# Product 4 of the first layer through seven products of its own blocks

## The chip, the cores and the metric

The kernel runs on one core of a Trainium2 chip. The metric is device time in microseconds (us) of one execution; lower is better. Five engines work side by side, each through its own queue in order: TensorE (PE, matrix products; its weight loads are listed as PEld), VectorE (DVE), ScalarE (ACT), GpSimd (POOL, which also issues indirect DMAs) and SyncE (SP, which here only issues DMAs). Products are written to eight banks of 128x512 float32 in PSUM; everything else lies in SBUF. An instruction that needs another engine's result waits for it on a semaphore, and what stands behind it in its queue waits too.

## The reference

4096 tokens of 512 columns are rotated by quaternions (which reduces to a mixture of four blocks of 128 columns with 16 weights each) and sent through a mixture of 8 experts, two per token, with 1024 slots per expert.

```python
x_rotated = hamilton(q_left_n, hamilton(x_filtered, q_right_conj))
scores = softmax(xf @ gate_w.T);  topv, topi = top_k(scores, 2)
gates = topv / sum(topv)
disp[flat_idx] += xf * w                       # 8 experts x 1024 slots x 512
h = relu(einsum('ecd,ehd->ech', de, fc1_w) + fc1_b)     # 2048 hidden units
eo = einsum('ech,ehd->ecd', h, fc2_w) + fc2_b
out = x + sum(eo[flat_idx] * gates * w)
```

All data are float32. Most of the work is in the two products of each expert: 1024 slots x 512 x 2048, twice.

## The kernel before

After the routing (some 80 us, with the DMAs that it waits for) the kernel goes through 32 groups k = 4e+g: expert e, group g of 512 hidden units. A group's first layer multiplies weights (two blocks of 256 hidden units by two blocks of 256 columns) with slots (two halves of 512 slots). It does so by seven block products in place of eight (the form of Strassen and Winograd), numbered 0 to 6: left[i] is a block of the weights or a sum of blocks, right[i] a block or sum of blocks of the slots. `left1` makes four such sums per group on POOL, s0 to s3; `Slots.factors` makes four per expert, on POOL too (x0 to x3, 1024 columns each, by `sums`, lines 125 to 128). The results are four blocks of hidden units by slots, called h11, h21, h22 and r12, made of bank contents: product 0 with the bias gives h11; product 5 on top of it r12 and h21; 1 is added to h11; 6 to h21; 4 to h22 and to r12; 3 and 2 to h21 and r12.

Products 0, 5 and 4 are done directly (`half`, line 858): two halves m of 128 hidden units, two steps c of 128 columns, 128x512 each. Products 1, 6, 3 and 2 are done by seven products of their own blocks once more (`within`, line 837): 128x128 by 128x256, with sums of sums made by `left_sub` (POOL, lines 155 to 158, 128 columns each, four per group and product) and `right_sub` (DVE, lines 170 to 173, 256 columns each, four per expert and product). `pair` does two such products side by side, (1, 6) and (3, 2), so that one DVE addition (line 892) adds one bank to two result blocks; a bank t is accumulated on and read four times in turn, a bank u twice. Where a bank is written again, TensorE waits for the addition that reads it. After the two pairs, `chain` puts four DVE sums of 1024 columns (lines 820 to 825) at the front of the queue `background`; they make the left sides of the second layer.

The second layer (`second_layers`, `product2`, line 800) takes the group before, in two units of 256 slots, each with seven products of 128x128 by 128x256 four times, and additions into `acc` on DVE.

The order is written out by hand. The two generators are stepped in turn, 14 turns per group: a step of the first layer (for a direct product one half, for a pair two to four small products) and then one step of the second (one product). After each step `turn(n)` takes n entries of `background` (rotation of the next expert's slots, line 771 and the transposes of line 727; storing of results) and one of `fetches` (indirect gathers on POOL, lines 601, 633 and 694; exchanges of 32-column squares by SP, line 707, four DMAs an entry). `PACE` gives n by group, turn and generator. `TURN_OF_SUM` gives the turn of each of the four left sums, and the tuples behind `left_sub` and `right_sub` the turns of their four steps. The next expert's slots are gathered, exchanged, rotated and summed during groups 0 to 3 of the present one; its four sums x0 to x3 stand at turns 10 to 13 of group 3.

Memory for the hidden blocks: `beside` holds three blocks of a group next to each other (h11, h21, r12) in two copies, `unused` five single blocks, from which h22 and the sums of `chain` are taken and to which `product2` returns them.

Of the kernel before, what the change touches and what calls it, by code (L numbers as in the profile page):

```python
# [30 lines left out]
F32 = mybir.dt.float32  # L31
# [4 lines left out]
ALU = mybir.AluOpType  # L36
# [30 lines left out]
def kernel(  # L67
# [546 lines left out]
    beside = [hp.tile([P, 3, 2, HALF], F32, name=f"beside{i}") for i in range(2)]  # L614
    unused = [hp.tile([P, 2, HALF], F32, name=f"hidden{i}") for i in range(5)]
# [60 lines left out]
    class Slots:  # L676
# [37 lines left out]
        def arrivals(self, half):  # L714

            n = PER if half == 0 else 2
            t = self.a if half == 0 else self.b
            for at in range(0, PER, n):
                for st in range(n):
                    yield lambda st=st, at=at: self.gather_ahead(t[:, st], half, at + st)  # L720
                yield from [lambda: None] * 2
                for b in range(QT):
                    yield lambda b=b, at=at: self.exchange(t, half, at, b)
                yield from [lambda: None] * 2
# [71 lines left out]
    def product2(out, st0, factors, n, first, tiles=range(2)):  # L796
# [11 lines left out]
        if st0 + 2 == PER and 1 in tiles and n in (2, 3, 4, 5):  # L808
            unused.append(factors[0][n])

    def chain(k, h22):


        h11, h21, r12 = (beside[k % 2][:, i] for i in range(3))
# [3 lines left out]
        def last():  # L818
# [7 lines left out]
            *[lambda: None] * (2 if k == NK - 1 else 0),  # L826
            last,
        ]

# [16 lines left out]
    def layer1(k, factors, subs):  # L846
# [5 lines left out]
        h11, h21, r12 = (h[:, i] for i in range(3))  # L852
# [25 lines left out]
        def pair(n, o, at, base, base_read):  # L878

            two = h[:, at : at + 2]
            t, u = bank1(f"t{n}_{k}"), bank1(f"u{n}_{k}")
            halves = t.rearrange("p (n s) -> p n s", n=2)

            def both(bank, i, first=False):
                within(bank[:, A], subs, n, i, first)
                within(bank[:, B], subs, o, i)

            def add(m, half):  # L890
                to = two[:, :, m, half]
                V.tensor_tensor(to, halves, to, ALU.add)  # L892

            within(base[:, A], subs, o, 1)
            within(base[:, B], subs, o, 2)
            base_read()
            both(t, 0, True)
            add(0, A)
            yield
            both(t, 5)  # L900
            add(0, B)
            both(u, 4, True)
            to = two[:, :, :, B]
            term = u.rearrange("p (n s) -> p n s", n=2).unsqueeze(2).to_broadcast([P, 2, 2, HS])
            V.tensor_tensor(to, term, to, ALU.add)
            yield
            both(t, 6)
            add(1, B)
            within(u[:, A], subs, n, 1, True)
            within(u[:, B], subs, n, 2)  # L910
            V.tensor_tensor(two[:, 0, 0], u, two[:, 0, 0], ALU.add)
            yield
            both(t, 3)
            add(1, A)
            relu(two[:, 0])

        def from5(m):
            nc.scalar.activation(h21[:, m], a[m], AF.Identity, bias=hi[:, m : m + 1])

        def from4(m):  # L920
            V.tensor_tensor(r12[:, m], b[m], r12[:, m], ALU.add)

        yield from pair(1, 6, 0, a[0], lambda: from5(0))
        yield
        h22 = unused.pop(0)
        b = [bank1(f"b{m}_{k}") for m in range(2)]
        for m in range(2):
            half(b[m], m, 4, True)
            V.tensor_tensor(h22[:, m], b[m], h21[:, m], ALU.add)
            if m == 1:  # L930
                from4(1)
                relu(h22)
            yield
# [378 lines left out]
```

## Time and profile before

| | us |
|---|---|
| median of 3 runs (lowest to highest) | 1564.13 (1563.52 to 1565.92) |
| the profiled execution, whole | 1567.49 |
| its span, first to last instruction | 1565.7 |
| VectorE busy | 1152.8 |
| GpSimd busy | 1045.9 |
| one group of hidden units (stretch from 360.50 to 407.00) | 46.5 |

A profile's page gives busy time by engine, the chain of work that ended last, and groups of equal instructions: line, engine, operation, output from inputs, shape, count, then busy us and mean ns of one, then the engine's idle us in front of them with what ended it. Answers in order of time have the start in us, the duration in us, engine, line, operation and what it writes from what; in square brackets the idle time before and who ended it. A float32 product appears as two passes. Consecutive passes overlap in this list, so a pass's cost is the distance between starts and not its duration.

### The profile page before, as it was taken

To read this page: it belongs to the slowest core of one execution; us is meant where nothing else is said; L and a number is where in the kernel's file an instruction comes from. 1 tells how busy PE (TensorE), PEld (TensorE's weight loads), DVE (VectorE), ACT (ScalarE), POOL (GpSimd) and SP (SyncE) were. 2 spreads that over 40 slices of the span, in tenths; PEclk is the share of its full clock that TensorE was granted. 3 is DMA by queue.
4 is the path that set the end of the run, shared out by engine and by line. 5 is a ranking of instruction groups with operands and counts; after the bars stand their busy time and mean duration, and the time that the engine had idled before them with its cause. 6 is when DMAs were issued, how large, how long until landed. Compare 5 with 4: busy or idle time off the path is not lost.

```text
span 1565.7 us, 17505 instructions
## 1 busy us (share of the span) xinstructions
PE 1531.0 (98%) x6399; PEld 1186.9 (76%) x6399; DVE 1152.8 (74%) x1608; ACT 316.6 (20%) x446; POOL 1045.9 (67%) x1129
## 2 busy tenths in 40 slices
PE   5899999999999999999999999999999999999997
PEld 2677777877877777877877777887777877777776
DVE  6667887588866888578885888758886688866656
ACT  3222211211131211221122221221212211121110
POOL 1763687755977478865779567785687747886453
PEclk7899999999999999999999999999999999999999
DMA  8463113421335203441135311442123511321021
GB/s 325 150 215 101 55 61 122 121 81 55 96 106 144 65 28 114 124 118 55 54 95 166 96 55 32 137 130 86 55 79 115 145 41 55 114 94 67 0 82 53
DMA packets 79374, 152.18 MB, mean 97 GB/s; under 512 B 12022, under 2 KB 40950, under 8 KB 74168
## 3 DMA queue, kind: packets, MB, share of 16 engines
q1 hardware_dynamic: 56848, 90.24, 18.6%
q0 software_dynamic: 18048, 52.31, 10.8%
q10 hardware_dynamic: 4392, 8.52, 1.4%
q8 instruction: 50, 0.82, 0.2%
q14 instruction: 36, 0.29, 0.1%
HBM read 119.77 MB, written 25.23 MB: 93 GB/s over the span
## 4 chain that ended last, share of the span: by engine, by line
PE 87%; DVE 6%; DMA 2%; issue 2%; POOL 1%; another core or an unknown queue 1%; SPq 1%; POOLq 0%; DVEq 0%
PE a L800 26%; PE b L800 19%; PE t L837 13%; PE a L858 11%; PE u L837 7%; PE b L858 7%; PE b L837 2%; PE a L837 1%; DMA xb<-in_xt_dram 1%; DVE hidden L824 1%; DVE xa L771 1%; PE p L959 1%; DVE hidden L820 1%; SPq L707 1%
## 5 line engine op out<-in xcount | busy, mean ns | idle before, releaser
L800 PE MATMUL a<-t,hidden 128*128 128x256 f32 x1024 | 242.0, 379 | 0.1
L892 DVE TENSOR_TENSOR beside<-t,beside 128x512 f32<-128x512 f32 x248 | 170.3, 687 | 92.3 <-PE t L837 88.1
L800 PEld LDWEIGHTS a<-t,hidden 128*128 128x128 f32 x1024 | 194.5, 190 | 53.0 <-issue 27.5
L833 ACT ACTIVATE beside<-beside 128x1024 f32<-128x1024 f32 x62 | 65.5, 1057 | 556.8 <-DVE beside L892 535.1
L837 PE MATMUL t<-xsub,sub 128*128 128x256 f32 x496 | 128.1, 381 | 0.9 <-DVE beside L892 0.2
L800 PEld LDWEIGHTS b<-w,hidden 128*128 128x128 f32 x504 | 95.8, 190 | 39.0 <-issue 29.2
L800 PE MATMUL b<-w,beside 128*128 128x256 f32 x512 | 121.0, 379 | 0.6 <-DVE acc L1224 0.6
L800 PE MATMUL a<-t,beside 128*128 128x256 f32 x512 | 120.9, 379 | 0.0
L800 PE MATMUL a<-w,beside 128*128 128x256 f32 x512 | 120.9, 379 | 0.0
L800 PE MATMUL b<-t,hidden 128*128 128x256 f32 x504 | 119.1, 379 | 0.0
L800 PE MATMUL b<-w,hidden 128*128 128x256 f32 x504 | 119.1, 379 | 0.0
L800 PEld LDWEIGHTS b<-w,beside 128*128 128x128 f32 x512 | 97.2, 190 | 27.3 <-issue 15.8
L800 PEld LDWEIGHTS a<-w,beside 128*128 128x128 f32 x512 | 97.3, 190 | 26.4 <-issue 14.8
L858 PE MATMUL b<-x,s 128*128 128x512 f32 x248 | 116.5, 592 | 0.0
L858 PE MATMUL a<-x,s 128*128 128x512 f32 x248 | 116.5, 592 | 0.0
L858 PE MATMUL a<-xa,w 128*128 128x512 f32 x248 | 116.4, 592 | 0.0
L137 POOL TENSOR_TENSOR s<-w 128x512 f32<-128x512 f32 x31 | 39.5, 1274 | 112.5 <-PE b L858 112.5
L139 POOL TENSOR_TENSOR s<-w 128x512 f32<-128x512 f32 x31 | 39.7, 1282 | 109.7 <-PE t L837 109.6
L140 POOL TENSOR_TENSOR s<-w,s 128x512 f32<-128x512 f32 x31 | 39.4, 1272 | 107.5 <-PE t L837 96.7
L800 PEld LDWEIGHTS a<-t,beside 128*128 128x128 f32 x512 | 97.3, 190 | 13.2
L837 PEld LDWEIGHTS t<-xsub,sub 128*128 128x128 f32 x496 | 93.6, 190 | 16.3 <-DVE beside L892 3.4
L800 PEld LDWEIGHTS b<-t,hidden 128*128 128x128 f32 x504 | 95.8, 190 | 13.0
(228 smaller groups left out, 3084.9 us busy)
## 6 DMA issues: line engine op xcount, KB each, us to landing
w<-in_w_dram SPq DMA_DIRECT2D x64, 1024.0 KB
xb<-in_xt_dram SPq DMA_DIRECT2D x8, 1024.0 KB
out_dram<-in_x_dram ACTq DMA_DIRECT2D x1, 8192.0 KB
rows<-xa SPq DMA_DIRECT2D x112, 64.0 KB
rows<-xb SPq DMA_DIRECT2D x224, 32.0 KB
b<-in_b_dram POOLq DMA_DIRECT2D x8, 256.0 KB
c<-choice,slot_cho POOLq DMA_INDIRECT x64
rows<-out_dram,slot_tok POOLq DMA_INDIRECT x64
```

The source lines that it names most:

```text
L137: lambda: G.tensor_tensor(s[0], w[:, 1, 0], w[:, 1, 1], ALU.add),
L139: lambda: G.tensor_tensor(s[2], w[:, 0, 0], w[:, 1, 0], ALU.subtract),
L140: lambda: G.tensor_tensor(s[3], w[:, 0, 1], s[1], ALU.subtract),
L707: nc.sync.dma_start(slots_of[half][q * CW : (q + 1) * CW, at : at + t.shape[1], b * P : (b + 1) * P], t[b * CW : (b + 1) * CW, :, q * P : ...
L771: V.scalar_tensor_tensor(to, t, M[:, i, j : j + 1], to, ALU.mult, ALU.add)
L800: nc.tensor.matmul(out[m] if isinstance(out, list) else out[:, m], lhsT=factors[0][n][:, c, (st0 + m) * P : (st0 + m + 1) * P], rhs=factor ...
L820: V.tensor_tensor(s4, h21, s2, ALU.subtract)
L824: lambda: V.tensor_tensor(s2, s1, h11, ALU.subtract),
L833: nc.scalar.activation(h, h, AF.Relu)
L837: nc.tensor.matmul(out, lhsT=subs[0][n][i], rhs=subs[1][n][i], start=first, stop=True, skip_group_check=True,)
L858: nc.tensor.matmul(out, lhsT=factors[0][n][:, c, m * P : (m + 1) * P], rhs=factors[1][n][:, c, :], start=first and c == 0, stop=c == 1, sk ...
L892: V.tensor_tensor(to, halves, to, ALU.add)
```

## The change

Product 4 is taken out of the direct products. Its blocks now come from `left_sub` and `right_sub` too (four more sums of 128 columns on POOL per group, four more of 256 columns on DVE per expert), and it is done by `within` in seven products of 128x128 by 128x256. Two banks serve it: b takes products 1 and 2 of its blocks (and afterwards those of product 2), t4 the others, its first half in four steps one after the other, its second half in one. h22 becomes a fourth block of `beside`, so that one DVE addition of a t4 half reaches h22 and r12 together (`add_to_both`); ACT copies the second half of h21 to h22 beforehand. In turn 9 both products into t4 stand in front of the additions that read them.

Around it: `unused` shrinks from five blocks to three; the last sum of `chain` is held in `waiting` until the second layer's unit returns its block, after that unit's product 2; left sums 0 and 1 move to turns 11 and 12, since s0 is read until turn 11; the steps of `left_sub` and `right_sub` are placed anew (in an expert's first group the sums of slots stand in turns 2 to 10); gathers and exchanges of the next expert are appended part by part at the turns of `ARRIVE`, and its rotation starts at turn 7 of group 1 and turn 6 of group 2; `PACE` is rewritten, and group 1 of the whole run uses the row of its own position.

```diff
-    beside = [hp.tile([P, 3, 2, HALF], F32, name=f"beside{i}") for i in range(2)]
-    unused = [hp.tile([P, 2, HALF], F32, name=f"hidden{i}") for i in range(5)]
+    beside = [hp.tile([P, 4, 2, HALF], F32, name=f"beside{i}") for i in range(2)]
+    unused = [hp.tile([P, 2, HALF], F32, name=f"hidden{i}") for i in range(3)]
...
-        def arrivals(self, half):
+        def arrive(self, half, part):
...
-            for at in range(0, PER, n):
-                for st in range(n):
-                    yield lambda st=st, at=at: self.gather_ahead(t[:, st], half, at + st)
-                yield from [lambda: None] * 2
-                for b in range(QT):
-                    yield lambda b=b, at=at: self.exchange(t, half, at, b)
-                yield from [lambda: None] * 2
+            at = part // 2 * n
+            if part % 2 == 0:
+                return [
+                    lambda st=st: self.gather_ahead(t[:, st], half, at + st) for st in range(n)
+                ]
+            return [lambda b=b: self.exchange(t, half, at, b) for b in range(QT)]
...
-        if st0 + 2 == PER and 1 in tiles and n in (2, 3, 4, 5):
+        if st0 + 2 == PER and 1 in tiles and n in (2, 4, 5):
...
-    def chain(k, h22):
-        h11, h21, r12 = (beside[k % 2][:, i] for i in range(3))
+            if n == 2 and waiting:
+                background.insert(0, waiting.pop())
+    waiting = []
+    def chain(k):
+        h11, h22, h21, r12 = (beside[k % 2][:, i] for i in range(4))
...
-            *[lambda: None] * (2 if k == NK - 1 else 0),
-            last,
...
+        (waiting if k else background).append(last)
...
-        def pair(n, o, at, base, base_read):
...
-        def from5(m):
-            nc.scalar.activation(h21[:, m], a[m], AF.Identity, bias=hi[:, m : m + 1])
-        def from4(m):
-            V.tensor_tensor(r12[:, m], b[m], r12[:, m], ALU.add)
-        yield from pair(1, 6, 0, a[0], lambda: from5(0))
+        def singles(bank, n, first=False):
+            within(bank[:, A], subs, n, 1, first)
+            within(bank[:, B], subs, n, 2)
+        def both(bank, n, o, i, first=False):
+            within(bank[:, A], subs, n, i, first)
+            within(bank[:, B], subs, o, i)
+        def add(two, m, half, bank):
+            to = two[:, :, m, half]
+            V.tensor_tensor(to, bank.rearrange("p (n s) -> p n s", n=2), to, ALU.add)
+        def add_twice(two, bank):
+            to = two[:, :, :, B]
+            term = bank.rearrange("p (n s) -> p n s", n=2).unsqueeze(2).to_broadcast([P, 2, 2, HS])
+            V.tensor_tensor(to, term, to, ALU.add)
+        def add_to_both(two, m, half, term):
+            to = two[:, :, m, half]
+            V.tensor_tensor(to, term.unsqueeze(1).to_broadcast([P, 2, HS]), to, ALU.add)
+        def add_pair(one, bank):
+            V.tensor_tensor(one[:, 0], bank, one[:, 0], ALU.add)
+        two = h[:, 0:3:2]
+        t, u = bank1(f"t1_{k}"), bank1(f"u1_{k}")
+        singles(a[0], 6)
+        nc.scalar.activation(h21[:, 0], a[0], AF.Identity, bias=hi[:, 0:1])
+        both(t, 1, 6, 0, True)
+        add(two, 0, A, t)
...
-        h22 = unused.pop(0)
-        b = [bank1(f"b{m}_{k}") for m in range(2)]
-        for m in range(2):
-            half(b[m], m, 4, True)
-            V.tensor_tensor(h22[:, m], b[m], h21[:, m], ALU.add)
-            if m == 1:
-                from4(1)
-                relu(h22)
-            yield
-        yield from pair(3, 2, 1, b[0], lambda: from4(0))
-        chain(k, h22)
+        both(t, 1, 6, 5)
+        add(two, 0, B, t)
+        both(u, 1, 6, 4, True)
+        add_twice(two, u)
+        yield
...
+        nc.scalar.activation(h22[:, 1], h21[:, 1], AF.Copy)
+        two = h[:, 1:4:2]
+        b, t4 = bank1(f"b_{k}"), bank1(f"t4_{k}")
+        singles(b, 4, True)
+        V.tensor_tensor(h22[:, 0], b, h21[:, 0], ALU.add)
+        within(t4[:, A], subs, 4, 0, True)
+        add_to_both(two, 0, A, t4[:, A])
+        yield
+        within(t4[:, A], subs, 4, 5)
+        within(t4[:, B], subs, 4, 4)
+        add_to_both(two, 0, B, t4[:, A])
+        to = two[:, :, :, B]
+        term = t4[:, B].unsqueeze(1).unsqueeze(1).to_broadcast([P, 2, 2, HS])
+        V.tensor_tensor(to, term, to, ALU.add)
+        yield
+        three = h[:, 2:4]
+        t, u = bank1(f"t3_{k}"), bank1(f"u3_{k}")
+        singles(b, 2)
+        within(t4[:, A], subs, 4, 6)
+        add_to_both(two, 1, B, t4[:, A])
+        both(t, 3, 2, 0, True)
+        add_pair(r12, b)
+        add(three, 0, A, t)
+        yield
+        within(t4[:, A], subs, 4, 3)
+        add_to_both(two, 1, A, t4[:, A])
+        relu(h22)
+        both(t, 3, 2, 5)
+        add(three, 0, B, t)
+        both(u, 3, 2, 4, True)
+        add_twice(three, u)
+        yield
...
+        relu(h21)
+        chain(k)
...
-        TURN_OF_SUM = {8: 2, 9: 0, 10: 1, 13: 3}
+        TURN_OF_SUM = {8: 2, 11: 0, 12: 1, 13: 3}
...
+        ARRIVE = (
+            {
+                (0, 5): [(0, 0)],
+                (1, 0): [(0, 1)],
+                (1, 2): [(1, 0)],
+                (1, 5): [(1, 1)],
+                (1, 9): [(1, 2)],
+                (1, 12): [(1, 3)],
+            },
+            {
+                (0, 3): [(0, 0)],
+                (0, 6): [(1, 0)],
+                (0, 13): [(0, 1)],
+                (1, 6): [(1, 1)],
+                (1, 10): [(1, 2)],
+                (1, 13): [(1, 3)],
+            },
+        )
...
-                    (2, left_f[2], (2, 2, 3, 3)),
-                    (3, w1_of[k][:, 1, 1], (4, 4, 5, 5)),
+                    (4, left_f[4], (2, 2, 3, 3)),
+                    (2, left_f[2], (4, 4, 5, 5)),
+                    (3, w1_of[k][:, 1, 1], (6, 6, 7, 7)),
...
-                    for n, turns in ((6, (1, 2, 2, 3)), (2, (4, 4, 5, 5)), (3, (6, 7, 8, 9))):
+                    for n, turns in (
+                        (6, (2, 2, 3, 3)),
+                        (4, (3, 4, 4, 5)),
+                        (2, (2, 4, 7, 10)),
+                        (3, (3, 5, 8, 10)),
+                    ):
...
-                        lefts[6], more = left_sub(k + 1, 6, left_n[6])
-                        later(more, (9, 10, 11, 12))
-                        lefts[1], more = left_sub(k + 1, 1, w1_of[k + 1][:, 0, 1])
-                        later(more, (10, 11, 12, 13))
+                        for n, block, turns in (
+                            (1, w1_of[k + 1][:, 0, 1], (8, 8, 9, 9)),
+                            (6, left_n[6], (9, 10, 10, 11)),
+                        ):
+                            lefts[n], more = left_sub(k + 1, n, block)
+                            later(more, turns)
...
-                            later(more, (8, 9, 9, 12))
+                            later(more, (8, 10, 10, 12))
...
-                    if (g, i) in ((0, 12 if e else 5), (1, 8)):
-                        fetches.extend(nxt.arrivals(g))
-                    if (g, i) in ((1, 11), (2, 9)):
+                    for part in ARRIVE[e > 0].get((g, i), ()):
+                        fetches.extend(nxt.arrive(*part))
+                    if (g, i) in ((1, 7), (2, 6)):
...
-        [(1, 1)] * 2 + [(0, 1)] * 4 + [(0, 0)] + [(0, 1)] * 5 + [(1, 1), (0, 0)],
-        [(1, 1)] * 4 + [(1, 1), (0, 2), (0, 0), (0, 1), (1, 1)] + [(0, 1)] * 3 + [(1, 1), (0, 0)],
-        [(1, 1)] * 2 + [(2, 1)] * 2 + [(1, 2), (0, 2), (0, 0), (0, 1), (1, 1)]
-        + [(0, 1)] * 3 + [(1, 1), (0, 0)],
+        [(1, 1)] * 2 + [(1, 1)] * 4 + [(0, 0)] + [(0, 1)] * 5 + [(1, 1), (0, 0)],
+        [(1, 1)] * 4 + [(1, 2), (0, 2), (0, 0), (0, 1), (0, 1), (0, 0), (1, 1), (0, 0), (1, 1), (0, 0)],
+        [(1, 1)] * 2 + [(2, 1)] * 2 + [(1, 2), (1, 1), (0, 0), (0, 1), (0, 1), (0, 0), (1, 1), (0, 0), (1, 1), (0, 0)],
...
```

More of the change, by code (lines that the diff above doesn't have):

```diff
@@ L851, in layer1 @@
         h = beside[k % 2]
-        h11, h21, r12 = (h[:, i] for i in range(3))
+        h11, h22, h21, r12 = (h[:, i] for i in range(4))
         A, B = slice(0, HS), slice(HS, HALF)
@@ L876, in layer1 @@
             yield
-        def pair(n, o, at, base, base_read):
[L882 to L898, printed above, removed]
-            yield
-            both(t, 5)
-            add(0, B)
-            both(u, 4, True)
+        def singles(bank, n, first=False):
+            within(bank[:, A], subs, n, 1, first)
+            within(bank[:, B], subs, n, 2)
@@ L903, in pair @@
+        def both(bank, n, o, i, first=False):
[5 more added lines that the diff above has]
+        def add_twice(two, bank):
             to = two[:, :, :, B]
-            term = u.rearrange("p (n s) -> p n s", n=2).unsqueeze(2).to_broadcast([P, 2, 2, HS])
+            term = bank.rearrange("p (n s) -> p n s", n=2).unsqueeze(2).to_broadcast([P, 2, 2, HS])
@@ L905, in pair @@
             V.tensor_tensor(to, term, to, ALU.add)
[L906 to L915, printed above, removed]
-        def from5(m):
-            nc.scalar.activation(h21[:, m], a[m], AF.Identity, bias=hi[:, m : m + 1])
-        def from4(m):
-            V.tensor_tensor(r12[:, m], b[m], r12[:, m], ALU.add)
@@ L923, in layer1 @@
-        yield from pair(1, 6, 0, a[0], lambda: from5(0))
-        yield
-        h22 = unused.pop(0)
-        b = [bank1(f"b{m}_{k}") for m in range(2)]
-        for m in range(2):
-            half(b[m], m, 4, True)
-            V.tensor_tensor(h22[:, m], b[m], h21[:, m], ALU.add)
-            if m == 1:
-                from4(1)
-                relu(h22)
-            yield
-        yield from pair(3, 2, 1, b[0], lambda: from4(0))
-        chain(k, h22)
+        def add_to_both(two, m, half, term):
+            to = two[:, :, m, half]
+            V.tensor_tensor(to, term.unsqueeze(1).to_broadcast([P, 2, HS]), to, ALU.add)
@@ new lines, in add_pair @@
+        def add_pair(one, bank):
[6 more added lines that the diff above has]
+        add(two, 0, A, t)
+        yield
+        both(t, 1, 6, 5)
[3 more added lines that the diff above has]
+        yield
+        both(t, 1, 6, 6)
@@ new lines, in layer1 @@
+        add(two, 1, B, t)
+        singles(u, 1, True)
+        add_pair(h11, u)
+        yield
+        both(t, 1, 6, 3)
+        add(two, 1, A, t)
+        relu(h11)
+        yield
[7 more added lines that the diff above has]
+        yield
@@ new lines, in layer1 @@
+        add_pair(r12, b)
+        add(three, 0, A, t)
+        yield
+        within(t4[:, A], subs, 4, 3)
[5 more added lines that the diff above has]
+        add_twice(three, u)
+        yield
+        both(t, 3, 2, 6)
+        add(three, 1, B, t)
+        singles(u, 3, True)
+        add_pair(h21, u)
+        yield
+        both(t, 3, 2, 3)
+        add(three, 1, A, t)
+        relu(h21)
+        chain(k)
@@ L943, in layer1_plain @@
         lo, hi = (b1_sb[:, e, g * 4 + 2 * a : g * 4 + 2 * a + 2] for a in range(2))
-        h11, h21, r12 = (beside[k % 2][:, i] for i in range(3))
-        h22 = unused.pop(0)
+        h11, h22, h21, r12 = (beside[k % 2][:, i] for i in range(4))
         for half in range(2):
@@ L977, in layer1_plain @@
                 if half == 1 and done:
-                    chain(k, h22)
+                    chain(k)
                 if len(parts) == 1 or i % 2:
@@ L1263 @@
                 k, i = now
-                turn(1 if k in (0, NK - 1) else PACE[0 if k == 1 else min(k % NG, 2)][i][n])
+                turn(1 if k in (0, NK - 1) else PACE[min(k % NG, 2)][i][n])
         while background:
```

## The prediction

> **What bounds the kernel now.** I read the page first (shares, slices, chain), then the waits of TensorE (PE), then four equal stretches that hold the four hidden groups of one expert, last the order of time at the places that the change touches.
>
> ```profile
> PE 1531.0 (98%) x6399; PEld 1186.9 (76%) x6399; DVE 1152.8 (74%) x1608; ACT 316.6 (20%) x446; POOL 1045.9 (67%) x1129
> ...
> PE 87%; DVE 6%; DMA 2%; issue 2%; POOL 1%; another core or an unknown queue 1%; SPq 1%; POOLq 0%; DVEq 0%
> ...
> L892 DVE TENSOR_TENSOR beside<-t,beside 128x512 f32<-128x512 f32 x248 | 170.3, 687 | 92.3 <-PE t L837 88.1
> ```
>
> TensorE is busy 98% of the span and carries 87% of the chain. The idle slices lie at the two ends. VectorE (DVE) mostly waits for it: the additions of line 892 stood idle 88.1 us for the bank they read.
>
> ```profile
> 313.70:360.50 46.80, 46.68 (x192) 36.04 (x191) 39.39 (x52) 9.51 (x13) 23.69 (x28) 1.00 0.26 83
> 360.50:407.00 46.50, 46.50 (x193) 36.42 (x192) 39.72 (x53) 7.19 (x9) 35.85 (x35) 1.00 0.15 48
> 407.00:453.70 46.70, 46.70 (x194) 36.55 (x193) 35.69 (x50) 9.75 (x13) 37.02 (x39) 1.00 0.33 106
> 453.70:500.40 46.70, 46.70 (x194) 36.60 (x193) 27.04 (x36) 12.17 (x18) 36.20 (x41) 1.00 0.48 131
> ```
>
> Columns after the stretch: length, then busy us of PE, PEld, DVE, ACT, POOL, then the granted clock. These are groups 2, 3, 0, 1 of an expert. TensorE fills each at clock 1.00; DVE needs 27 to 40 of some 46.6 us. So a TensorE pass taken away shortens the run, as long as no new wait appears on it. Waits of that kind are rare now, but DVE and GpSimd (POOL) hold each other up, which makes the next block the one to read:
>
> ```profile
> 313.39 1.89 PE L800 MATMUL a<-w,beside 128*128 128x256 f32 x8
> 315.12 1.88 PE L858 MATMUL a<-xa,w 128*128 128x512 f32 x4
> 315.93 2.98 DVE L824 TENSOR_TENSOR hidden<-hidden,beside 128x1024 f32<-128x1024 f32 x1
> 316.54 1.28 POOL L125 TENSOR_TENSOR t<-w 128x512 f32<-128x512 f32 x1
> ...
> 329.18 0.73 PEld L837 LDWEIGHTS t<-xsub,sub 128*128 128x128 f32 x4 [0.52 <-DVE beside L892]
> ...
> 384.04 1.27 POOL L139 TENSOR_TENSOR s<-w 128x512 f32<-128x512 f32 x1 [3.29 <-PE t L837]
> 385.52 1.88 PE L858 MATMUL b<-x,s 128*128 128x512 f32 x4
> 385.72 0.69 DVE L1141 TENSOR_TENSOR v<-a,acc 128x512 f32<-128x512 f32 x1 [0.57 <-PE a L800]
> 386.32 0.74 DVE L771 SCALAR_TENSOR_TENSOR xc<-xps,M,xc 128x512 f32<-128x512 f32 x1
> 388.04 0.41 DVE L170 TENSOR_TENSOR xsub<-xa 128x256 f32<-128x256 f32 x1
> ...
> 400.90 2.36 POOL L127 TENSOR_TENSOR x<-xb,xc 128x1024 f32<-128x1024 f32 x1
> 401.85 1.69 DVE L173 TENSOR_TENSOR xsub<-xa,xsub 128x256 f32<-128x256 f32 x1
> ```
>
> The DVE operation at 401.85 takes both inputs from SBUF. Alone its kind takes 0.41 us (388.04); begun 0.95 us into a 2.36 us POOL sum it took 1.69, that is 1.28 more. L824 at 315.93 likewise ended 1.09 us after the POOL sum that began at 316.54. The lateness that L824 starts is still there at 329.18, where TensorE waits.
>
> **The change, part by part.**
>
> *TensorE.* From the x8 row one 256-column pass takes (1.89-0.379)/7 = 0.216 us (0.379 is the mean of one in its group), from the x4 row one 512-column pass (1.88-0.592)/3 = 0.430. A float32 product is two passes. Product 4 was 4 products of 512 columns, 8 x 0.430 = 3.44 us; it becomes 7 of 256, 14 x 0.216 = 3.02. That is 0.41 us in each of 31 groups: **-12.8 us**, all on the path.
>
> A page speaks against this term. The Trainium skill, "TensorE: Matmul & The Clock Gate", section "Back-to-back issue gap", gives a sustained 81 ns for 128 columns and 131 ns for 512, so that halving the columns would not halve the time; between those two figures 14 short passes would cost about a third more than 8 long ones, and the change would lose. The two rows of this case scale with the columns (0.216 against 0.430), and the rows decide.
>
> *VectorE, in sum.* Product 4's four additions (lines 929, 921) become seven: six of 512 elements and one of 1024. By 687 ns (line 892) and 1225 ns (line 905, same shape) that is 5.35 - 2.75 = 2.6 us more per group, and four more operand sums per expert, 1.7 us alone. The stretches go from 39.4, 39.7, 35.7, 27.0 to about 42, 42.3, 40, 29.6 of 46.2 us: DVE does not become the bound by its sum. ACT gains one copy of 512 elements per group (0.69 us, the form of line 869) in a queue busy 7 to 12 of 46 us: nothing. POOL gains four 128-column sums per group (0.46 us, line 158): 1.7 us in stretches of 24 to 37. The pair-1/6 chain and the pair-3/2 chain keep their instructions. The gathers and exchanges move earlier; SP's queue and POOL's indirect issues keep their number, POOL waits for exchanges moves by turns, and the 16 issues of an exchange (0.60 us each, line 707) take 9.6 of the four turns (13 us) before the gather that waits for them: nothing, and if that cover is gone POOL stops for the rest of a transfer (2.56 us before the gather at 314.03), in front of its sums. A wait of SP for a scatter would hold the weight loads behind it; those are issued at turns 0 and 3, half a group before they are read.
>
> *The last sum of a hidden block* is issued after the preceding unit's product 2, so one operation of 1.22 us leaves the crowded first turns of each group. Its reader is the last product of the next unit, seven turns later: nothing, and without those turns 1.22 us per group.
>
> *The old stall.* At the turn of group 2 two gathers of POOL (314.03, 315.57) push its weight sums onto L824; TensorE then loses 0.37 us at 329.18 (eight passes from 327.18 are through at 328.91, and the next four take 1.13 us instead of 1.03) and 0.17 us at 333.67 (0.07 and 0.10 by the same count), in six experts: 3.3 us. In the new order the second pair of gathers stands at turn 10 of group 1, three turns earlier, so the pile-up is not made: **-3.3 us**; bounds 0 and -3.3. The value is the far end because group 3, which has the same sums and no gathers, shows no such wait.
>
> *A new stall in group 3.* Product 4's middle uses one bank (t4) four times in turn; each reuse waits for the addition before it. I count from product 4's first pass (385.52 in the row above). TensorE reaches the third use of t4 after 6+8+4+8+4 passes, at 30 x 0.216 = 6.48 us. VectorE's queue up to the addition it waits for, back to back (starts 0.61 apart for 512 elements, 0.66 for line 771, 0.33 for an operand sum, all from neighbouring starts; 0.73 where the next reads the result): v at 0.20, weighted add 0.80, h22 add 1.46, first t4 add 2.18, operand sum of product 1 (moved here) 2.79, acc add 3.23 (its product ends then), weighted add 3.84, t4 add 4.50, broadcast add 5.22, ended 6.45. It is just in time, with no slack. But POOL: s2 begins 1.48 us before the zero (384.04), then 1.23 and five 128-column sums 0.42 apart, so the first 1024-column operand sum (line 125, 2.35 us) runs from about 1.9 to 4.26. The DVE operand sum arrives at 2.79, 0.9 into it: the geometry of 401.85. It costs 1.28, of which 0.1 falls into a wait that was there; with the 0.1 us by which a first weight load is late after a wait, TensorE loses 1.3 us, once per expert but the last: 7 x 1.3 = **+9.1 us**. Bounds: 0 (POOL later by more than 0.9, so that DVE goes first) and 7 x 2.4 (the full POOL sum).
>
> That POOL and DVE exclude each other for a whole instruction is also what "SBUF — State Buffer", section "Who interferes with whom", states for a DVE operation with two SBUF inputs. It is the rule that speaks against this placement; the row agrees (1.69 against 0.41).
>
> *Small waits at t4 in groups 1 and 2*, where the same count leaves some 0.1 us because rotation steps of 0.72 to 0.74 us stand in the queue: bounds 0 and 0.17 (the loss at 333.67) at two places in 14 groups, 4.8 us; I take 0.1 at one: **+1.4 us**.
>
> Sum: -12.8 -3.3 +9.1 +1.4 = **-5.6 us**. The profiled execution took 1567.49 us (span 1565.7 and 1.8 around it), 3.4 above the median of 1564.13; so it becomes 1561.9, and the median **1558.5**.
>
> **Rivals.**
>
> *No collision.* POOL's queue comes late (eight choice gathers and four new sums stand in front; the 3.29 us wait at 384.04 shrinks) and DVE's operand sum goes first: -12.8 -3.3 +1.4 = -14.7, **1549.4**. Against it: 3.29 us covers the 1.7 us of new sums.
>
> *Waits remain everywhere.* The old stall stays, and each of 31 groups loses 0.17 at one place: -12.8 +9.1 +5.3 = +1.6, **1565.7**, no measurable change. For it: slack near zero at t4.
>
> *Slower: a second collision per expert*, in group 0, where sixteen DVE operand sums and POOL's part sums run in the same turns 2 to 10. At 1.3 us each: -5.6 +9.1 = +3.5, **1567.6**. It decides from 19.2 us of new stalls (12.8+3.3+3.1), 2.7 us per expert. For it: operand sums of 1.5 us instead of 0.41 occur there now; against it: they cost TensorE nothing so far.
>
> *The change doesn't do what it says*: short passes do not take half the time. Then -12.8 is lost and the run is at about 1571. The rows at 313.39 and 315.12 exclude nearly all of it.
>
> **How the numbers follow.** Forecast 0.49, no collision 0.17, waits everywhere 0.18, second collision 0.13, no gain 0.03. 0.2% is 3.1 us, about what can be told from no change. Faster: the first two, 0.66; same: 0.19; slower: 0.15. The range runs from just below the no-collision case, 1548.5, to the second collision, 1568; the forecast alone has 1554 to 1562.
>
> **What would show it.** Right: line 800's pass times unchanged; TensorE waits for t4 about 1.3 us seven times, some 187 us apart, each with an operand sum of about 1.7 us and a 1024-column POOL sum before it; the 0.52 us wait at the third group gone. Wrong: no wait at t4 (no collision), waits at t1 or u early in an expert (second collision), or a DVE that lags through whole groups.

## The result and the profile after

| | before | after |
|---|---|---|
| median, us (lowest to highest) | 1565.03 (1563.52 to 1567.59) | 1576.38 (1575.28 to 1578.01) |
| the profiled execution, whole | 1567.49 | 1575.28 |
| its span | 1565.7 | 1573.5 |
| ratio after / before, 95% interval | | 1.0072 (1.0054 to 1.0089) |

The changed kernel is slower by 11.3 us; the forecast was 5.6 us faster (1558.5, range to 1568). The page of the kernel after, its shares, its granted clock by slice, its chain and the two groups of product 4:

```profile
PE 1520.8 (97%) x6585; PEld 1223.2 (78%) x6585; DVE 1235.1 (78%) x1733; ACT 332.1 (21%) x477; POOL 1107.0 (70%) x1253
...
PEclk7889999999999999999999999999999999999999
...
PE 89%; DVE 6%; DMA 2%; POOL 1%; another core or an unknown queue 1%; SPq 1%; issue 1%; POOLq 0%; DVEq 0%
...
L840 PE MATMUL t<-xsub,sub 128*128 128x256 f32 x682 | 181.2, 385 | 20.6 <-DVE beside L901 13.3
...
L901 DVE TENSOR_TENSOR beside<-t,beside 128x512 f32<-128x512 f32 x124 | 85.0, 685 | 17.6 <-PE t L840 13.9
```

TensorE is busy 10.2 us less than before (1520.8 against 1531.0) and the span is 7.8 us longer: the products did get shorter, and TensorE stands more. Of its 20.6 us of waiting at line 840, 13.3 have one releaser, the addition of line 901 into the shared bank t4. Whether that is many short waits or a long one shows in the distance between the first passes of product 0 of consecutive groups, read from the starts of TensorE's rows. Only the first row of the table starts earlier: it takes in the last 32 passes of group 0 (line 992), which need 13.7 us in both kernels, and ends at product 0 of k = 2. "The stretch k = 1" means this one below.

| group | before, us | after, us |
|---|---|---|
| k = 1, the first group with all parts, and the end of group 0 | 57.18 | 71.56 |
| group 1 of a later expert | 46.56 | 46.15 to 46.31 |
| group 2 | 47.12 | 46.36 |
| group 3 | 46.56 | 47.65 |
| group 0 | 46.56 | 46.15 to 46.28 |

The windows of the kernel after, for k = 1 and then groups 1, 2, 3 of the second expert and group 0 of the third (columns as before: length, busy us of PE, PEld, DVE, ACT, POOL, granted clock):

```profile
66.80:138.30 71.50, 58.37 (x215) 41.86 (x214) 43.61 (x66) 13.95 (x21) 34.71 (x37) 0.90 0.51 168
278.50:324.70 46.20, 46.20 (x200) 37.63 (x199) 32.61 (x41) 12.59 (x19) 38.58 (x46) 1.00 0.45 130
324.70:371.00 46.30, 46.30 (x199) 37.41 (x198) 39.40 (x52) 10.06 (x15) 22.33 (x29) 1.00 0.18 58
371.00:418.70 47.70, 46.60 (x200) 37.47 (x200) 41.67 (x54) 7.75 (x11) 37.43 (x40) 1.00 0.14 44
418.70:465.00 46.30, 46.30 (x200) 37.65 (x199) 38.36 (x56) 10.31 (x15) 41.75 (x47) 1.00 0.45 139
```

After the first expert all groups but group 3 got shorter; a clean one takes 46.15 us, 0.41 less than 46.56. From k = 2 to the last group but one the kernel after needs 1351.0 us against 1353.6. The loss, 14.4 us, is all in k = 1, where the clock granted over the stretch is 0.90 and TensorE idles 13 us. The rows there, in order of time (weight loads left out):

```profile
104.64 0.59 PE L840 MATMUL t<-x,s 128*128 128x256 f32 x2
105.08 1.89 PE L800 MATMUL a<-t,beside 128*128 128x256 f32 x8
109.84 6.38 SPq L707 DMA_DIRECT2D rows<-xa  x10
116.34 10.18 SPq L707 DMA_DIRECT2D rows<-xb  x16
117.94 0.73 DVE L727 STREAM_TRANSPOSE xps<-rows 128x512 f32<-128x512 f32 x1 [13.27 <-DMA rows<-xa]
118.58 0.66 DVE L933 TENSOR_TENSOR beside<-b,beside 128x512 f32<-128x512 f32 x1
...
119.35 0.69 DVE L901 TENSOR_TENSOR beside<-t,beside 128x512 f32<-128x512 f32 x1
...
120.09 2.08 PE L840 MATMUL t<-xsub,sub 128*128 128x256 f32 x4 [13.13 <-DVE beside L901]
...
121.96 2.73 PE L800 MATMUL b<-w,hidden 128*128 128x256 f32 x8
...
128.62 0.99 POOL L694 DMA_INDIRECT xb<-in_xq_dram,slot_tok  x1 [23.61 <-DMA rows<-xb]
```

Read it from the bottom of the queue up. VectorE's first transpose of the next expert (line 727) waits 13.27 us for an exchange; behind it in VectorE's queue stand the two additions of product 4 (lines 933 and 901); TensorE waits 13.13 us for the second. The eight passes at 121.96 then take 2.73 us where the same row takes 1.89. The addition is the releaser that the profile names, but the one that is late is the exchange. SP's own waits between 60 and 140 us say why:

```profile
SPq L707 <- DMA out_dram<-in_x_dram: 13.6, 1, 13.6
```

(total, times, longest.) SP stands 13.6 us, until its row at 109.84, for the copy of x to out: 8 MB, one DMA, issued in group 0. Before the change SP waited 13.7 us for the same copy, but the transpose came four turns later, at 121.39, and waited 1.4 us, behind which TensorE ran on. The two rows of the kernel before:

```profile
SPq L707 <- DMA out_dram<-in_x_dram: 13.7, 1, 13.7
```

```profile
121.39 0.73 DVE L727 STREAM_TRANSPOSE xps<-rows 128x512 f32<-128x512 f32 x1 [1.44 <-DMA rows<-xb]
```

What ties an exchange to a copy whose data it does not touch stands in the packed trace, which holds for each DMA the semaphore that tells of its landing and those that it waits for. The DMAs of SP and ScalarE take their landing semaphores in turn from eight (100, 102, 103, 105, 107, 108, 109, 110), and nearly every one waits, before it is issued, for the DMA that had the same semaphore last. The copy (issued at 57.67) has 110. The first six DMAs of the next expert's exchanges have 102 to 109 and are issued by 95.63; the seventh is the next to have 110, waits for that semaphore alone, and is issued at 109.84. Before the change it is the seventh too, at 112.17.

The other lines that the prediction named: in group 3 the operand sum of line 170 meets GpSimd's 1024-column sum, as forecast.

```profile
399.75 2.36 POOL L125 TENSOR_TENSOR x<-xc,xa 128x1024 f32<-128x1024 f32 x1
400.07 0.69 DVE L901 TENSOR_TENSOR beside<-t,beside 128x512 f32<-128x512 f32 x1
400.68 1.72 DVE L170 TENSOR_TENSOR xsub<-xa 128x256 f32<-128x256 f32 x1
...
405.63 0.70 PE L840 MATMUL t<-xsub,sub 128*128 128x256 f32 x2 [1.10 <-DVE beside L942]
```

### The profile page after: what moved, and what is told of

It reads as the page before. It is cut to its first block, busy times and chain, and to the rows that moved or that the text cites. A ratio compares the mean times of both kernels' runs of the same rounds, so it can differ in the third digit from the quotient of the medians.

```text
span 1573.5 us, 18187 instructions
## 1 busy us (share of the span) xinstructions
PE 1520.8 (97%) x6585; PEld 1223.2 (78%) x6585; DVE 1235.1 (78%) x1733; ACT 332.1 (21%) x477; POOL 1107.0 (70%) x1253
## 4 chain that ended last, share of the span: by engine, by line
PE 89%; DVE 6%; DMA 2%; POOL 1%; another core or an unknown queue 1%; SPq 1%; issue 1%; POOLq 0%; DVEq 0%
PE a L800 26%; PE b L800 20%; PE t L840 17%; PE a L861 13%; PE u L840 7%; PE b L840 3%; PE a L840 2%; DMA xb<-in_xt_dram 1%; DVE xb L771 1%; PE p L992 1%; DVE xsub L170 1%; DVE beside L901 1%; SPq L707 1%; DVE beside L942 1%
## 5 line engine op out<-in xcount | busy, mean ns | idle before, releaser
L800 PE MATMUL a<-t,beside 128*128 128x256 f32 x1024 | 242.1, 379 | 0.1
L891 DVE TENSOR_TENSOR beside<-t,beside 128x512 f32<-128x512 f32 x248 | 170.4, 687 | 73.2 <-PE t L840 69.8
L800 PEld LDWEIGHTS a<-t,beside 128*128 128x128 f32 x1024 | 194.9, 190 | 39.3 <-issue 14.3
L840 PE MATMUL t<-xsub,sub 128*128 128x256 f32 x682 | 181.2, 385 | 20.6 <-DVE beside L901 13.3
L840 PEld LDWEIGHTS t<-xsub,sub 128*128 128x128 f32 x682 | 127.5, 191 | 45.2 <-DVE beside L901 18.0
L800 PE MATMUL a<-t,hidden 128*128 128x256 f32 x512 | 121.0, 379 | 0.0
L137 POOL TENSOR_TENSOR s<-w 128x512 f32<-128x512 f32 x31 | 39.6, 1278 | 114.3 <-PE t L840 114.3
L800 PEld LDWEIGHTS b<-w,hidden 128*128 128x128 f32 x504 | 96.7, 192 | 26.0 <-issue 13.1
L800 PEld LDWEIGHTS a<-t,hidden 128*128 128x128 f32 x512 | 97.5, 190 | 13.0
L800 PEld LDWEIGHTS b<-t,hidden 128*128 128x128 f32 x504 | 95.9, 190 | 12.8
L901 DVE TENSOR_TENSOR beside<-t,beside 128x512 f32<-128x512 f32 x124 | 85.0, 685 | 17.6 <-PE t L840 13.9
L657 POOL DMA_INDIRECT out_dram<-rows,slot_add x64 | 71.2, 1113 | 37.5 <-DVE rows L652 17.5
L155 POOL TENSOR_TENSOR sub<-w 128x128 f32<-128x128 f32 x62 | 37.0, 597 | 73.2 <-PE u L840 72.7
## 6 DMA issues: line engine op xcount, KB each, us to landing
xb<-in_xt_dram SPq DMA_DIRECT2D x8, 1024.0 KB, 13.3
```

The source lines that it names most:

```text
L137: lambda: G.tensor_tensor(s[0], w[:, 1, 0], w[:, 1, 1], ALU.add),
L155: lambda: G.tensor_tensor(t[:, 0], b(1, 0), b(1, 1), ALU.add),
L657: nc.gpsimd.indirect_dma_start(out=out_of[st], out_offset=bass.IndirectOffsetOnAxis(ap=slot_add[:, s : s + 1], axis=0), in_=self.rows[st], ...
L800: nc.tensor.matmul(out[m] if isinstance(out, list) else out[:, m], lhsT=factors[0][n][:, c, (st0 + m) * P : (st0 + m + 1) * P], rhs=factor ...
L840: nc.tensor.matmul(out, lhsT=subs[0][n][i], rhs=subs[1][n][i], start=first, stop=True, skip_group_check=True,)
L891: V.tensor_tensor(to, bank.rearrange("p (n s) -> p n s", n=2), to, ALU.add)
```

## The experiments

Theory A: two placements cost, independently of each other. The transpose moved to turn 7 puts a wait for an exchange that is late behind the 8 MB copy in front of product 4's additions, once (13.3 us and 1.9 us of slow passes after it); and the collision in group 3 costs 1.37 us in seven experts. Rival B: VectorE has too much to do (82 us more busy), and a wait taken out comes back. Rival C: SP's queue is late by itself, with or without the copy.

Each run was measured beside the kernel before on the same chip; the ratio is to that. The column before the last is the ratio less the changed kernel's 1.0072, times 1565 us; the interval of 1.0072 alone is 2.7 us to either side. The last column is read from the rows of one execution each: the distance from product 0 of k = 1 to that of the last group (1408.9 us in the changed kernel, 1397.1 before), which leaves out the start and the end of the run (80.2 to 82.7 us and 84.1 to 88.3 us in these executions, without relation to the edits). The two runs on the kernel before are compared with that kernel there.

| run | median, us | before there | ratio, 95% interval | against after, us | by rows, us |
|---|---|---|---|---|---|
| rotation later | 1571.62 | 1568.72 | 1.0020 (1.0011 to 1.0029) | -8.1 | -5.0 |
| copy later | 1563.06 | 1568.72 | 0.9965 (0.9951 to 0.9978) | -16.7 | -14.6 |
| sum at turn 9 | 1569.89 | 1568.72 | 1.0007 (0.9998 to 1.0016) | -10.2 | -10.7 |
| copy and sum | 1554.29 | 1568.72 | 0.9910 (0.9895 to 0.9926) | -25.4 | -23.8 |
| before, copy later | 1564.42 | 1564.47 | 1.0003 (0.9994 to 1.0012) | | -0.4 |
| before, early rotation | 1573.45 | 1564.47 | 1.0055 (1.0041 to 1.0069) | | +10.6 |
| slot sums from turn 11 | 1583.73 | 1564.47 | 1.0118 (1.0103 to 1.0134) | +7.2 | +7.0 |
| rotation and gathers later | 1561.63 | 1564.47 | 0.9981 (0.9972 to 0.9990) | -14.2 | -14.3 |

### The copy later

```diff
-                    nc.scalar.dma_start(*(a.rearrange("(b r) d -> r b d", r=PT) for a in (out, x)))
+                if k == 2 and i == 3:
+                    nc.scalar.dma_start(*(a.rearrange("(b r) d -> r b d", r=PT) for a in (out, x)))
```

> The changed kernel, with the copy of x to out (8 MB, one DMA on ScalarE's queue at turn 1 of group 0) issued at turn 3 of group 2 instead; the rotation stays at turn 7. Theory A (the exchange is late because SP stands 13.6 us for that copy): SP's wait goes, the stall at 120 us goes, 15.2 us less: 1561 us. Rival C (SP's queue is late by itself, or the gathers are): the stall stays at 10 us or more, 1572 us or more. A third way: the copy runs later beside weight loads of 5 us each and holds up SP there: the stall comes back in group 2 or 3 at the same size, some 1570 to 1576 us.

Measured: 16.7 us less than the changed kernel (14.6 by the rows), for an expected 15.2. The stretch k = 1 takes 56.46 us in place of 71.56, which is 15.1. The transpose, still at turn 7, does not wait at all, and TensorE runs through the same place:

```profile
102.61 9.54 SPq L707 DMA_DIRECT2D rows<-xb  x15
...
106.63 0.72 DVE L727 STREAM_TRANSPOSE xps<-rows 128x512 f32<-128x512 f32 x1
...
107.25 0.67 DVE L933 TENSOR_TENSOR beside<-b,beside 128x512 f32<-128x512 f32 x1
...
108.03 0.69 DVE L901 TENSOR_TENSOR beside<-t,beside 128x512 f32<-128x512 f32 x1
...
108.84 1.06 PE L840 MATMUL t<-xsub,sub 128*128 128x256 f32 x4
```

The early transpose is harmless once SP does not stand behind the copy; Rivals B and C fall. SP's wait for the copy appears nowhere later in this run, so the third way falls as well: the copy now takes semaphore 103 at 137.53, and the next DMA with it is issued at 277.6. With the copy out of the way, the change is worth 0.9965, or 5.5 us less than before (2.9 less by the rows).

### The first expert's rotation later

```diff
-                    if (g, i) in ((1, 7), (2, 6)):
+                    if (g, i) in ((1, 7 if e else 11), (2, 6)):
...
-                turn(1 if k in (0, NK - 1) else PACE[min(k % NG, 2)][i][n])
+                turn(1 if k in (0, NK - 1) else PACE[min(k % NG, 2)][i][n] + (k == 2 and n == 1 and i < 9))
```

> The changed kernel, with the first expert's rotation started at turn 11 of group 1 again, as before the change, and one more entry taken from background at nine turns of group 2 so that it is through in time. Theory A (VectorE's first transpose, moved up four turns, stands in front of product 4's additions and waits for an exchange that is late): the single stall of 13.3 us at 120 us goes, and with it some 1.9 us of passes at half pace behind it, so 15.2 us less than 1576.4: 1561 us, and the transpose waits about 1.4 us or not at all. Rival B (the loss lies in VectorE's additional 82 us of work spread over all groups, and a wait taken out in one place comes back in the next): at most 5 us less, 1571 us or more. Rival C (the first expert's exchange is late because SP's own queue is fuller): as A here, and told apart by the next kernel.

Measured: 8.1 us less by the ratio and 5.0 by the rows, a third to a half of what was expected. The median, 1571.62, lies where Rival B put it; the rows say why it is not B. VectorE's transpose (119.64) no longer waits, and k = 1 takes 56.53 us, 15.0 less; but k = 2 now takes 56.62 in place of 46.36:

```profile
129.45 1.14 POOL L694 DMA_INDIRECT xb<-in_xq_dram,slot_tok  x1 [24.50 <-DMA rows<-xb]
130.23 0.69 DVE L1283 TENSOR_TENSOR acc<-a,b 128x512 f32<-128x512 f32 x1 [0.48 <-PE a L800]
130.84 0.72 DVE L727 STREAM_TRANSPOSE xps<-rows 128x512 f32<-128x512 f32 x1
130.90 0.95 POOL L694 DMA_INDIRECT xb<-in_xq_dram,slot_tok  x1 [0.30 <-issue]
...
134.44 1.26 POOL L138 TENSOR_TENSOR s<-s,w 128x512 f32<-128x512 f32 x1
135.75 3.78 PE L861 MATMUL a<-x,s 128*128 128x512 f32 x4 [5.55 <-POOL s L138]
```

The same late exchanges have a second waiter. GpSimd's second gather, moved to turn 9, overwrites the buffer that the exchange before it still reads; it stands 24.5 us, and the weight sums of the next group (lines 137, 138) stand behind it. In the changed kernel that wait is there too (23.61 us, the last row at k = 1 above), but TensorE was held longer by VectorE, so it did not show. Taking one waiter away uncovered the other: 5.55 us of wait and then four passes in 3.78 us where they take 1.88. What came back is not VectorE's work but a second wait for the same transfers.

### Rotation and gathers later

The edit above, and in the first expert's table of arrivals:

```diff
-                (1, 2): [(1, 0)],
-                (1, 5): [(1, 1)],
-                (1, 9): [(1, 2)],
-                (1, 12): [(1, 3)],
+                (1, 8): [(1, 0)],
+                (1, 10): [(1, 1)],
+                (1, 13): [(1, 2)],
+                (2, 1): [(1, 3)],
```

> The changed kernel, with the first expert's rotation at turn 11 as in the first experiment and also its second half's gathers and exchanges later (gathers at turns 8 and 13 of group 1, exchanges at turn 10 and at turn 1 of group 2, where the changed kernel has 2, 9, 5 and 12). Theory A2 (the one late exchange has two waiters: VectorE's transpose, and GpSimd's second gather, which stood 24.5 us in front of the weight sums and cost 5.6 us at product 5 and some 1.8 us of passes at half pace in the first experiment): both waits go, 15 to 17 us less than the changed kernel, as with the copy moved. Rival (the rest of the first experiment's loss is not the gather's): about 8 us less, as there.

Measured: 14.2 us less. VectorE's transposes wait nowhere and GpSimd's gather 4.6 us, behind which TensorE does not stand, although SP still waits 11.6 us for the copy. The k = 1 stretch takes 56.43 us; 1.8 us of the missing ones are in k = 2 (48.20), where TensorE loses 0.4 to 0.8 us at three places (145.04, 146.37, 158.97). The first experiment has the same three; that they come from the additional entries of background is likely and was not tried alone. So the loss has two waiters and one late transfer, and either end mends it.

### One part alone, on the kernel before

```diff
-                    if (g, i) in ((1, 11), (2, 9)):
+                    if (g, i) in ((1, 11 if e else 7), (2, 9)):
```

> The kernel before, with only the first expert's rotation started at turn 7 of group 1 in place of turn 11; product 4, arrivals and sums as they were. Theory A (the early transpose alone makes the loss): VectorE waits some 13 us for the first expert's exchange, TensorE behind it 10 to 14 us, and some 1.9 us at half pace follow: 12 to 16 us more than the kernel before. Rival (the loss needs product 4's additions, which stand behind the transpose and have only one bank to go round, so that without them TensorE runs on): less than 5 us more.

Measured: 1.0055, some 9.0 us more by the medians (6.4 to 10.8 by the interval) and 10.5 by the length of k = 1 (67.67 against 57.18). Less than expected, since TensorE does not stop as early:

```profile
107.66 1.88 PE L858 MATMUL b<-x,s 128*128 128x512 f32 x4
109.37 1.89 PE L800 MATMUL b<-w,hidden 128*128 128x256 f32 x8
...
117.72 0.73 DVE L727 STREAM_TRANSPOSE xps<-rows 128x512 f32<-128x512 f32 x1 [12.62 <-DMA rows<-xa]
118.36 0.67 DVE L929 TENSOR_TENSOR hidden<-b,beside 128x512 f32<-128x512 f32 x1
...
119.08 1.22 PE L837 MATMUL b<-xb,s 128*128 128x256 f32 x2 [7.82 <-DVE hidden L929]
```

VectorE waits 12.6 us, much as in the changed kernel, TensorE 7.8 and not 13.1. The direct product 4 writes two banks once each, so TensorE could go on to 111.3; t4 is read before it is written again, and TensorE stopped at 107.0. So the rival is right in part: the early transpose makes the wait, and the new product 4 takes away some 5 us of the distance that would have absorbed it.

The copy moved in the kernel before (the same edit as above) was expected to do nothing:

> The kernel before, with only the copy of x to out moved from turn 1 of group 0 to turn 3 of group 2. Theory A (the late exchange costs only where an instruction reaches it before the copy has landed, and before the change the first transpose came 1.4 us too early, behind which TensorE did not wait): between 0 and 2 us less than the kernel before. Rival (the copy slows the first expert in general, whatever the order of VectorE): 5 us less or more, and then the 16.8 us (1.07%) that moving it gave the changed kernel is not the price of the change's earlier rotation.

Measured: 1.0003 (0.9994 to 1.0012), nothing. The copy costs only what is put in front of its end.

### The collision in group 3

```diff
-                            later(more, (8, 10, 10, 12))
+                            later(more, (9, 10, 10, 12))
```

> The changed kernel, with only the first step of the sums of slots for product 1 moved from turn 8 to turn 9 of group 3 (a VectorE sum of 256 columns, from in front of t4's second addition to behind it). Theory A (that sum meets GpSimd's first sum of 1024 columns and waits for its end, and TensorE loses 1.26 + 0.11 us at t4 in seven groups): 9.6 us less, 1566.8 us, groups of 47.65 us become 46.3, the stall of 13 us at 120 us stays. Rival B (VectorE's queue in that turn is simply full): the wait moves to the next addition, 47.65 us becomes 47.2 or more, 1573 us or more.

Measured: 10.2 us less (10.7 by the rows). Group 3 takes 46.39 us in place of 47.65, 1.26 less in six experts and 1.00 in the seventh, 8.6 us in all, and no other group got longer. Of the rest 1.9 us are not the edit's: the stall in the first expert stays, but TensorE waits 11.4 us there in this execution and not 13.1. The sum alone, behind t4's additions:

```profile
402.35 0.41 DVE L170 TENSOR_TENSOR xsub<-xa 128x256 f32<-128x256 f32 x1
```

This run moves both the sum's place in VectorE's queue and its time, so the next leaves VectorE's order alone and moves GpSimd's sums:

```diff
-                if k and fill_n and i >= 10:
+                if k and fill_n and i >= 11:
                     assert nxt.rotated == 2 * NJ
-                    fill_n.pop(0)()
+                    for _ in range(1 + (i == 13)):
+                        fill_n.pop(0)()
```

> The changed kernel, with GpSimd's four sums of 1024 columns put at turns 11, 12, 13, 13 of group 3 instead of 10 to 13; VectorE's order is untouched, the sum of 256 columns stays in front of t4's second addition. Theory A (VectorE's sum takes 1.72 us only because it meets GpSimd's): it takes 0.41 us, groups of 47.65 us become 46.3 to 46.4, 9.6 us less than the changed kernel, with up to 2.4 us per expert given back if GpSimd, late by one sum, holds up the next group. Rival (its place in VectorE's queue is the cause): groups of 47.65 us stay.

Measured: group 3 takes 46.39 us here too, with VectorE's sum where it was:

```profile
403.58 0.69 DVE L901 TENSOR_TENSOR beside<-t,beside 128x512 f32<-128x512 f32 x1
404.19 0.42 DVE L170 TENSOR_TENSOR xsub<-xa 128x256 f32<-128x256 f32 x1
...
425.19 2.30 DVE L828 TENSOR_TENSOR hidden<-hidden,beside 128x1024 f32<-128x1024 f32 x1
...
426.37 2.24 POOL L125 TENSOR_TENSOR t<-w 128x512 f32<-128x512 f32 x1
427.41 2.28 DVE L829 SCALAR_TENSOR_TENSOR beside<-beside 128x1024 f32<-128x1024 f32 x1
```

0.42 us at the same place in the queue, so it was the meeting and not the place. But the run as a whole is 7.2 us slower than the changed kernel: group 0 of the next expert grew from 46.2 to some 48.5 us (47.97 in the last), 2.2 us on average in seven experts. That is more than the sum gained, and it lies at the far end of what was expected (7 x 2.4 less 9.6 is 7.2).

GpSimd, late by one sum, now lies beside other operations of VectorE. In the changed kernel the same two sums of `chain` read:

```profile
422.94 1.22 DVE L828 TENSOR_TENSOR hidden<-hidden,beside 128x1024 f32<-128x1024 f32 x1
...
424.08 2.29 DVE L829 SCALAR_TENSOR_TENSOR beside<-beside 128x1024 f32<-128x1024 f32 x1
```

So line 829 met a GpSimd sum there already; what is new is line 828 (2.30 us for 1.22) and line 824 (2.11 at 433.64 for 1.35), and TensorE loses 1.2 us at a bank t, of which the profile counts 1.03 as idle:

```profile
439.36 1.13 PE L840 MATMUL t<-xsub,sub 128*128 128x256 f32 x4 [1.03 <-DVE beside L891]
```

It loses about 1 us more near the end of the group (462.98 and 464.21), after a sum of slots (line 173) took 2.63 us beside GpSimd's work at 458.07, for 1.63 in the changed kernel. This is close to the prediction's rival "a second collision per expert": the same group, and in part the same operand sums, but also the sums of `chain`, which it did not name. The links between these rows are read from their order and were not tried one by one.

### Both, and the best version

> Both edits at once: copy at turn 3 of group 2, first step of product 1's sums of slots at turn 9. Theory A: the two losses are independent and add up, -15.2 and -9.6 from 1576.4: 1551.6 us, below the kernel before (1565.0) by 13.4, of which 12.8 is the shorter product 4. Rival B: 1565 us or more, since the shorter product 4 is eaten up by VectorE in any order.

```profile
L840 PE MATMUL t<-xsub,sub 128*128 128x256 f32 x682 | 180.1, 383 | 2.3 <-issue 2.2
```

Measured: 0.9910 (0.9895 to 0.9926), 14.4 us less than the kernel before on that chip (1554.29 against 1568.72), and 25.4 less than the changed kernel for an expected 24.8. By the rows it is 23.8, which is the sum of the two parts there (15.1 of the stall and 8.6 of group 3). TensorE's waits at line 840 went from 20.6 to 2.3 us. This version beats both kernels: the change as it is, the copy issued two groups later, and one step of the sums of slots one turn later.

## Why the prediction was wrong

**The step that failed** is in the part on VectorE's sum: "The gathers and exchanges move earlier ... nothing, and if that cover is gone POOL stops for the rest of a transfer (2.56 us before the gather at 314.03), in front of its sums". It took the cover from a steady expert, where it holds for TensorE: after the change, line 727 waits once in the whole run, in the first expert, and the gathers of line 694 in five later places, 1.5 to 3.3 us each, behind which TensorE does not stand. In the first expert SP stood 13.7 us for the 8 MB copy before the change already, and the transpose's 1.4 us wait at 121.39 was in the trace of before: the exchange landed with no time to spare, and the start of the rotation was moved up four turns, some 13 us. The sentence counted SP's issues and GpSimd's gathers and left out the third queue that the step passes through, VectorE's, where the transposes stand in front of product 4's additions. It put this term at nothing; its price is 15.1 us (71.56 against 56.46 with the copy moved: 13.1 of wait at TensorE, the rest slow passes behind it). The bound given for the lost cover, 2.56 us, was a steady transfer's; the first expert's gather waited 23.6.

The other terms, by the rows:

- *TensorE, -12.8.* Right. A clean group is 46.15 us against 46.56, 0.41 as worked out. The rival that short passes do not take half the time is excluded, and the sustained figures that the prediction quotes do not hold for the float32 passes of this case.
- *The old stall, -3.3.* Right: the long group of 47.12 us became 46.36, which holds small waits only.
- *The new stall in group 3, +9.1.* Right in place and mechanism: 1.26 us in six experts, and in one 0.91 (1151.39) with 0.43 a turn before. With the sum moved the seven groups are 8.6 us shorter in all. The two runs on it show cause and size. That VectorE, with two inputs from SBUF, and GpSimd hold each other up for a whole instruction also agrees with "SBUF — State Buffer", section "Who interferes with whom", of the Trainium skill (0.42 us alone, 1.72 beside).
- *Small waits at t4, +1.4.* Too small: from k = 2 on the groups lie 12.7 us above 46.15 in all, and 4.1 of that is not the collision but many losses of some 0.1 us, spread over the groups of the first seven experts. Right in kind.
- *The rival with a second collision in group 0*: not in the changed kernel; something close to it appears when GpSimd is made one sum later.

Sum with the missing term: -12.8 - 3.3 + 8.6 + 4.1 + 15.1 = +11.7. The distance from the start of the stretch k = 1 to product 0 of the last group grew by 11.8 us (1410.8 to 1422.6). The spans differ by 7.8: in the execution after, that stretch begins 1.5 us earlier, and the end of the run from the last product 0 on takes 84.1 us against 86.6, most of which are losses of 2.0 us near 1514 and 1518 of before that have no counterpart.

With the copy moved, everything else as in the change, the run is 5.5 us faster than before by the ratio (3.5 to 7.7 by its interval). That this is next to the forecast's -5.6 is in part luck: without the stall the measured terms make -3.4, and the rows of that run give -2.9.

## What to carry to other kernels

A step that is moved earlier is covered only if its input is there, in each repetition of the loop: the first one, where setup transfers are still running, is read from its own rows and not from a steady one. A short wait in front of a step (here 1.4 us, costing nothing) says that it has no slack, and then every queue that the step passes is followed to what stands behind it. A wait for a transfer need not be a wait for its data: here it was for the semaphore that the transfer held. When a wait is removed and much of the loss stays, the same late transfer can have a second waiter.

## What was not expected of the hardware

After a long wait of TensorE the passes ran at half pace for a while. First two windows of the kernel after, from the end of its wait on, then one each of the early rotation alone and of the first experiment, which start 3.5 us after the end of theirs, then one of the best version (copy and sum) behind its wait of 2.2 us at 1500.84; the granted clock is the number after POOL's count in brackets:

```profile
120.09:123.30 3.21, 3.21 (x8) 2.58 (x9) 1.87 (x4) 1.03 (x2) 0.00 (x0) 0.50 0.24 51
123.50:130.00 6.50, 6.50 (x31) 5.68 (x31) 5.30 (x10) 0.00 (x0) 1.08 (x2) 0.99 0.15 31
```

```profile
122.60:125.00 2.40, 2.40 (x8) 1.90 (x7) 0.76 (x2) 0.19 (x1) 0.00 (x0) 0.57 0.23 47
```

```profile
139.30:142.00 2.70, 2.70 (x10) 2.15 (x9) 0.12 (x1) 0.69 (x1) 2.62 (x5) 0.76 0.23 49
```

```profile
1500.84:1503.00 2.16, 2.16 (x10) 1.93 (x11) 1.95 (x4) 0.00 (x0) 0.00 (x0) 1.00 0.06 23
```

In windows of half a microsecond the clock falls to 0.50 some 3.2, 3.4 and 3.7 us after TensorE's last pass in the first three of these runs. It is back at 1.00 some 3.6 us after the passes resume in the kernel after (wait of 13.1 us), 5.6 us in the early rotation alone (7.8 us) and 4.8 us in the first experiment (5.6 us). After 2.2 us of wait it stayed at 1.00. Half of the time at half pace is lost, so a wait of 5 us and more cost 1.8 to 2.8 us on top of itself here, and one of 2 us nothing. "TensorE: Matmul & The Clock Gate" of the Trainium skill, Part 1, "What's actually happening", says that the array falls to half its clock after an idle window of about 3.4 us and needs as long to come back. The fall agrees; the return took longer in two of the three runs.

The exchanges, moved earlier, also made SP wait for the stores of results (line 657): 279.2 us in 20 waits, up to 45.2 at a time, in the kernel after, against 7.0 in 2 before. The groups show no loss from it: after the first expert TensorE's waits of 0.1 us and more all lead to additions of VectorE.
